# A graph layer on one core: another order for the first blocks, a block's list by one product, and pieces of blocks placed by running sums

## The chip, the cores and the metric

One core of a Trainium2 chip runs the whole program. The metric is the device time of one execution in microseconds (us); a run's profile gives the span of the profiled execution and what each engine did in it. The engines are TensorE (PE; its weight loads are PEld), VectorE (DVE), ScalarE (ACT), GpSimd (POOL) and SyncE (SP). SP, ACT and POOL also issue DMAs.

## What is computed

A layer of a graph network over 12,500 nodes with 64 features and 212,500 edges; `row` holds the edges' sources, `col` their destinations. The edge list is sorted by destination.

```python
h = relu(layernorm(x))
edge_in = concat([h[row], h[col], dist], axis=1)
e = silu(edge_in @ eW1 + eb1)
e = silu(e @ eW2 + eb2)
agg = segment_sum(e, row, num_segments=12500)
out = silu(concat([h, agg]) @ nW1 + nb1) @ nW2 + nb2
return x + out
```

## The kernel before

**Tables.** The first edge product is taken per node, not per edge: `ta` holds the source half of `h @ eW1` for every node, `tb` the destination half, both in DRAM, each number split in two parts that add up. A small table `tb0` holds the destination half for the first 2,048 nodes only, so that the first blocks need not wait for the whole of `tb`. This bulk work (load x, `norm`, `products`) is cut into small parts by generators; `feed` hands out one part at a time, between other work.

**Blocks.** The edges are taken in 208 blocks of 1,024; two blocks (a pair) share one window of 60 or so neighbouring destination nodes, which suffices since the list is sorted. `destinations()` makes each pair's list: `rowsD` holds every edge's destination relative to the window, `base_i` where the window begins. `sources()` splits the source of each edge into its bucket (one of 100) and its place in the bucket, turned so that edges lie on partitions. A block then goes through

- `load`: SP loads the pair's window rows from the table (`win`, L360), and the two edge-weight rows (`extra`, L335);
- `spread` (L344): TensorE copies the pair's list row to 64 partitions, twice, once for each half of the block (`bc`);
- `count`: VectorE finds each edge's rank within its bucket (`oh` L387, `each` L395, `terms` L412, `rank` L414, `to`) with two products on TensorE, and makes the one-hot `pick` (L376);
- `send`: TensorE gathers by a product (`qp`, L454), ScalarE copies it to `qs` (L466, L469; eight buffers), and POOL scatters 128 edges at a time to the bucket's next rows in DRAM (`q`, L476). That is 8 scatters a block, 1,661 in all.

`send_all` runs `send(s)` beside `count(s+1)` and `load(s+2)` and yields three times a block; each of these thirds is a *piece*.

**Steps.** The rows of `q` are filled in 14 levels (`LEVELS`). When all blocks that can reach a level are sent, its rows are read again, 25 batches a level, bucket by bucket: 450 steps of 512 edges. A step makes a one-hot of the places (`one` L605), turns it (`lr` L562), adds the source half and the gathered half (`pt` L576, L583), applies silu (L592), the second edge product (L622), silu (L626) and the sum by node (`seg` L636, `aggT` L647). With the last level the node part (`nodes`) follows for each batch and the rows of the output go out.

**Order.** TensorE, VectorE, ScalarE and SP run their instructions in the order in which the program writes them; each waits in that order. At the start an explicit list `order` interleaves the generators; then eight blocks run with four parts of `feed` to a piece, then the pieces that level 0 needs with three. In the main loop a list `turn` gives the order within a step; at four places of it (`None`, the *hooks*) pieces are placed. `marks` says how many pieces must stand before which hook, so that a level's rows are complete before its first batch is loaded, three blocks ahead; between two marks the pieces are spread evenly over the hooks.

**The bias tile.** `b2f` holds eb2 four times over on all partitions. It is loaded after the eighth block (L855), spread by a product with ones (L858) and copied back (L859).

Of the kernel before, what the change touches and what calls it, by code (L numbers as in the profile page):

```python
# [28 lines left out]
F32 = mybir.dt.float32  # L29
# [10 lines left out]
P = 128  # L40
L = 125
WL = 60
# [20 lines left out]
FILL0, FILL_EACH, FILL_LATE = 22, 2, 8  # L63
AFTER = mybir.DependencyInfo(mybir.DependencyClass.Sync, mybir.DependencyReason.DATA)
# [13 lines left out]
def tile_gnn(ctx: ExitStack, tc: tile.TileContext, x, src, dst, ew, eW1, eb1, eW2, eb2, nW1, nb1, nW2, nb2, out):  # L78
# [48 lines left out]
    NE, EARLY = 16, 30  # L127
# [9 lines left out]
    dstR = lp.tile([NP, PAIR], I32, name="dstR")  # L137
    f, sf, t = (lp.tile([NP, PAIR], F32, name=n) for n in ("f", "sf", "t"))
    fv = f.rearrange("p (g e) -> p g e", e=HALF)
    lo = lp.tile([NP, 4], F32, name="lo")  # L140
    ewR, ewH = (lp.tile([NP, PAIR], F32, name=n) for n in ("ewR", "ewH"))
    nc.vector.memset(srcR[96:NP, LAST:], N)
    nc.vector.memset(ewR[96:NP, LAST:], 0.0)
    ones = const.tile([1, P], F32, name="ones")
# [3 lines left out]
    nc.sync.dma_start(x0, x[: NE * P, :].rearrange("(p j) d -> p j d", j=NE))  # L148
# [5 lines left out]
    for to, v, queue in ((srcR, src, nc.sync), (ewR, ew, nc.scalar), (dstR, dst, nc.sync)):  # L154
        for p0, p1 in ((0, 96), (96, NP - 1)):
            queue.dma_start(to[p0:p1, :], vec(v, p0 * PAIR, p1 - p0, PAIR))
        queue.dma_start(to[NP - 1 : NP, :LAST], vec(v, (NP - 1) * PAIR, 1, LAST))
    last = bass.AP(tensor=dst.tensor, offset=dst.offset + E - FEW, ap=[[PAD, 1], [0, PAD // FEW], [1, FEW]])
    nc.scalar.dma_start(dstR[NP - 1 : NP, LAST:].rearrange("p (r e) -> p r e", e=FEW), last)
# [25 lines left out]
    nc.vector.scalar_tensor_tensor(same, plus, -float(HB), part, op0=OP.mult, op1=OP.add)  # L185
    nc.vector.tensor_scalar(plus, same, float(WL + 2), None, op0=OP.is_equal)
# [20 lines left out]
    rowsD = const.tile([NP, 2, 2, HALF], BF16, name="rowsD")  # L207

    tb0 = dram.tile([P * NE, 2 * H], F32, name="tb0")
    ta_buckets, tb_buckets = (t.rearrange("(l b) f -> l b f", b=NB) for t in (ta, tb))  # L210
# [21 lines left out]
    base_i = const.tile([1, NP], I32, name="base_i")  # L232
    NW = 3
    wins = [const.tile([P, 2, 2, 2, H], F32, name=f"win{i}") for i in range(NW)]
    for win in wins:
        nc.vector.memset(win, 0.0)
# [15 lines left out]

    def later_weights():

        nc.gpsimd.dma_start(w2, eW2)
# [48 lines left out]
    with ExitStack() as work:  # L304
# [23 lines left out]
        def load_rows(s):  # L328

            if s < nblocks:  # L330
                p, g = s // 2, s % 2
                if g == 0:
                    for a in range(2):
                        at = a * HB + WL
                        nc.sync.dma_start(extras[p % 2][at : at + 2], ews[:, p, :, a])  # L335

        def spread(s):

            if s < nblocks:
                p, g = s // 2, s % 2  # L340
                bc = mm.tile([P, HALF], F32, name="bc", tag="mm")
                for a in range(2):
                    of = identb[:NP, p : p + 1].to_broadcast([NP, HB])
                    nc.tensor.matmul(bc[a * HB : (a + 1) * HB], of, rowsD[:, a, g], start=True, stop=True)  # L344
# [344 lines left out]
        def first_rows(g):  # L689
# [6 lines left out]
            nc.sync.dma_start(  # L696
                tb0.rearrange("(p j) f -> p j f", j=NE)[:, g : g + G, :], got.rearrange("p g k h -> p g (k h)")
            )
# [43 lines left out]
        def destinations():  # L742

            lim = lp.tile([NP, 1], F32, name="lim")
            nc.vector.tensor_scalar(lim, part[:NP], EARLY / 2 - 0.5, float((NB - NE) * P), op0=OP.is_gt, op1=OP.mult)
            nc.vector.tensor_scalar(lim, lim, float(NE * P - SPAN), None, op0=OP.add)
            nc.scalar.copy(f, dstR)
            yield
            nc.vector.tensor_scalar(lo[:, 0:1], fv[:, 0, 0:1], lim, None, op0=OP.min)
            lot = mm.tile([1, NP], F32, name="lot", tag="mm")  # L750
            nc.tensor.transpose(lot, lo[:, 0:1], ident[:NP, :NP])
            for h in range(1, 4):
                nc.vector.tensor_scalar(lo[:, h : h + 1], lo[:, 0:1], float(h * STEP), None, op0=OP.add)
            yield
            nc.scalar.copy(base_i, lot)
            for g in range(2):
                nc.vector.tensor_tensor(
                    rowsD[:, :, g, :],
                    fv[:, 2 * g : 2 * g + 2, :],
                    lo[:, 2 * g : 2 * g + 2, None].to_broadcast([NP, 2, HALF]),  # L760
                    op=OP.subtract,
# [30 lines left out]
        def checks():  # L792

            ends = lp.tile([NP, 2, 4], F32, name="ends")
            for i, (op, sign, limit) in enumerate(((OP.max, 1.0, WL - 0.5), (OP.min, -1.0, 0.5))):
                nc.vector.tensor_reduce(ends[:, i, :], fv, AX.X, op)
                nc.vector.tensor_tensor(ends[:, i, :], ends[:, i, :], lo, op=OP.subtract)
                nc.vector.tensor_scalar(ends[:, i, :], ends[:, i, :], sign, limit, op0=OP.mult, op1=OP.is_gt)
                yield
            nc.vector.tensor_reduce(bad[:NP, 0:1], ends.rearrange("p i g -> p (i g)"), AX.X, OP.max)  # L800
# [17 lines left out]
        with listing:  # L818
            todo = groups()
            for _ in range(2):  # L820
                list(todo.pop(0))
            lists_, rows_, src0, src1, weights = destinations(), norm(x0, NE), sources(0), sources(1), edge_weights()
            made = [first_rows(g) for g in range(0, NE, G)]
            next(rows_)
# [233 lines left out]
```

## Time and profile before

| | |
|---|---|
| median of three runs | 2402.55 us (2399.72 to 2406.02) |
| the profiled execution | 2402.95 us |
| its span | 2401.2 us |
| mean granted clock of TensorE | 0.915 |
| first scatter begins | 43.5 us |
| last scatter begins | 2209.2 us |

A page of the profile lists the busy time of each engine, the span in 40 equal slices (busy tenths), the chain of waits that ended last, and groups of instructions as `line engine op out<-in`, with busy time, mean ns, and idle time ahead with what ended it (`<-`). A view of stretches gives busy time (and count) by engine, the granted clock, the DMA engines' busy share and GB/s. The timeline gives start, duration, engine and instruction.

### The profile page before, as it was taken

The numbers are of one execution on the slowest core, as the hardware profiler recorded it, in microseconds if no ns is written. First come the engines' busy times: TensorE is split into PE (matmuls) and PEld (weight loads), VectorE is DVE, ScalarE is ACT, GpSimd is POOL, SyncE is SP. The second block draws the span as 40 slices with busy tenths as digits, with TensorE's granted clock in tenths as the row PEclk, the third lists the DMA queues.
The fourth block names the chain that finished last, engine by engine and source line by source line (L and its number), as shares of the span: only waits on it lengthen the run. The fifth ranks groups of instructions, "written<-read, shape, count | busy, mean of one in ns | idle before, by whom it ended". The sixth has DMA issues, their size and how long they took to land.

```text
span 2401.2 us, 47870 instructions
## 1 busy us (share of the span) xinstructions
PE 2084.7 (87%) x17025; PEld 1909.0 (80%) x17025; DVE 1807.1 (75%) x2852; ACT 1316.8 (55%) x2861; POOL 1655.6 (69%) x1723
## 2 busy tenths in 40 slices
PE   3777887666688889988999999999999999999997
PEld 2555676655588788888888999998999999999885
DVE  7989977766678787776877667899988888875221
ACT  3333444333355566656666767666666666666543
POOL 5667777777777777777777766777777777776110
PEclk9555698877889999999999999999999999999999
DMA  5565877666677666777777777988888888888663
GB/s 161 210 235 212 274 227 236 209 209 220 210 250 253 209 225 221 225 236 255 258 259 247 264 251 254 294 262 255 269 269 275 266 267 279 263 270 269 207 187 92
DMA packets 238859, 572.33 MB, mean 238 GB/s; under 512 B 46346, under 2 KB 98534, under 8 KB 238097
## 3 DMA queue, kind: packets, MB, share of 16 engines
q1 hardware_dynamic: 154598, 390.24, 51.8%
q0 software_dynamic: 54080, 124.64, 14.2%
q10 hardware_dynamic: 29936, 54.31, 6.9%
q8 instruction: 138, 2.26, 0.4%
q14 instruction: 107, 0.88, 0.1%
HBM read 356.62 MB, written 212.35 MB: 237 GB/s over the span
## 4 chain that ended last, share of the span: by engine, by line
PE 43%; DMA 19%; POOL 10%; DVE 7%; issue 5%; ACT 4%; SPq 1%; ACTq 0%; POOLq 0%; DVEq 0%
DMA q<-qs,to 16%; PE seg L636 10%; POOL q L476 10%; PE p L622 10%; PE pt L583 9%; PE pt L576 5%; PE qp L454 4%; PE lr L562 3%; DMA out_dram<-os 2%; PE bc L344 1%; ACT qs L466 1%; DVE one L605 1%; SPq L124 1%; ACT e L592 1%; DVE rank L414 1%
## 5 line engine op out<-in xcount | busy, mean ns | idle before, releaser
L476 POOL DMA_INDIRECT q<-qs,to x1661 | 1615.7, 973 | 565.5 <-issue 398.4
L583 PE MATMUL pt<-oneT,a 125*128 125x128 f32 (+1 forms) x2800 | 433.9, 293 | 143.1 <-ACT oneT L567 142.1
L592 ACT ACTIVATE e<-pt 128x512 f32<-128x512 f32 x450 | 268.8, 597 | 477.4 <-PE pt L583 471.9
L622 PE MATMUL p<-w,e 128*128 128x128 f32 x3600 | 513.4, 287 | 0.0
L636 PE MATMUL seg<-one,e 128*128 128x125 f32 x3600 | 508.9, 285 | 0.2 <-DVE aggT L647 0.2
L583 PEld LDWEIGHTS pt<-oneT,a 125*128 125x128 f32 x2800 | 365.8, 198 | 159.5 <-ACT oneT L567 157.8
L622 PEld LDWEIGHTS p<-w,e 128*128 128x128 f32 x3600 | 457.6, 198 | 22.4 <-issue 22.4
L636 PEld LDWEIGHTS seg<-one,e 128*128 128x128 f32 x3600 | 445.3, 195 | 28.7 <-issue 27.3
L466 ACT COPY qs<-qp 128x512 f32<-128x512 f32 x418 | 244.5, 586 | 392.3 <-DMA q<-qs,to 276.1
L647 DVE TENSOR_TENSOR aggT<-aggT,seg 128x500 f32<-128x500 f32 x325 | 218.5, 672 | 210.1 <-PE seg L636 208.0
L454 PE MATMUL qp<-win,pick 128*128 128x256 f32 x1664 | 329.1, 325 | 28.3 <-DVE pick L376 10.8
L605 DVE TENSOR_TENSOR one<-misc,qt 128x500 f32<-128x500 f32 x450 | 302.7, 673 | 60.0 <-PE seg L636 33.1
L395 DVE TENSOR_REDUCE each<-oh 128x100 bf16<-128x800 bf16 x208 | 321.1, 1544 | 7.2
L454 PEld LDWEIGHTS qp<-win,pick 128*128 128x128 f32 x1664 | 254.1, 213 | 48.2 <-issue 15.1
L576 PE MATMUL pt<-ident,qt 128*128 128x128 f32 x1800 | 276.5, 277 | 8.3 <-ACT qs L466 7.9
L626 ACT ACTIVATE e<-p 128x512 f32<-128x512 f32 x450 | 268.7, 597 | 25.6 <-PE p L622 25.2
L567 ACT CAST oneT<-lr 125x512 fp32r<-125x512 f32 x450 | 264.7, 588 | 12.8 <-PE lr L562 12.4
L616 ACT COPY p<-b2f 128x512 f32<-128x512 f32 x450 | 267.2, 594 | 0.0
L576 PEld LDWEIGHTS pt<-ident,qt 128*128 128x128 f32 x1800 | 209.6, 143 | 23.7 <-issue 12.2
L414 DVE TENSOR_REDUCE rank<-terms 128x8 f32<-128x864 f32 x208 | 219.0, 1053 | 7.2
L376 DVE SCALAR_TENSOR_TENSOR pick<-bc,same,extra 128x512 fp32r<-128x512 f32 x208 | 154.6, 743 | 82.4 <-PE bc L344 54.3
L412 DVE TENSOR_TENSOR terms<-oh,misc 128x800 f32<-128x800 bf16 x208 | 203.6, 979 | 6.2 <-PE misc L400 5.9
(142 smaller groups left out, 1662.8 us busy)
## 6 DMA issues: line engine op xcount, KB each, us to landing
a<-ta SPq DMA_DIRECT2D x350, 512.0 KB
qt<-q SPq DMA_DIRECT2D x250, 288.0 KB
qt<-q SPq DMA_DIRECT2D x100, 576.0 KB
q<-zeros ACTq DMA_DIRECT2D x25, 1080.0 KB
q<-qs,to POOLq DMA_INDIRECT x1661
win<-tb SPq DMA_DIRECT2D x208, 120.0 KB
tb<-got SPq DMA_DIRECT2D x29, 512.0 KB
q<-zeros ACTq DMA_DIRECT2D x20, 720.0 KB
```

The source lines that it names most:

```text
L395: nc.vector.tensor_reduce(each, oh.rearrange("p t b -> p b t"), AX.X, OP.add)
L454: nc.tensor.matmul(qp[:, t % 2, :k], halves(pick[:, t * P : (t + 1) * P]), halves(win[:, :k, v]), start=v == 0, stop=v == 1,)
L466: nc.scalar.copy(qs[:, ts, :k, :H], qp[:, ts, :k, :])
L476: ins = nc.gpsimd.indirect_dma_start(out=q[:], out_offset=bass.IndirectOffsetOnAxis(ap=to[:k, j : j + 1], axis=0), in_=qs[:k, t % 2, a, :] ...
L576: nc.tensor.matmul(pt[:, t, :], qt[:, j, :H], ident, is_transpose=True, start=t == 0, stop=False, skip_group_check=True)
L583: nc.tensor.matmul(pt[:, cols, :], halves(a[:L, b, i * H : (i + 1) * H]), halves(oneT[:, cols, :]), start=False, stop=i == 1, skip_group_c ...
L592: nc.scalar.activation(e1, pt, AF.Silu)
L605: nc.vector.tensor_tensor(one.rearrange("p (b j) l -> p b j l", j=n), spots[:, None, None, :].to_broadcast(wide), loc[:, tiles[0][1] : til ...
L616: nc.scalar.copy(p2, b2f)
L622: nc.tensor.matmul(p2[:, t, :], e1[:, t, :], w2, start=False, stop=t == G - 1, skip_group_check=True)
L626: nc.scalar.activation(e2, p2, AF.Silu)
L636: nc.tensor.matmul(item[2][:, b, :], e2[:, t, :], one[:, t, :], start=j < G, stop=j >= G * (n - 1))
```

## The change

*The start.* The rows of the first four groups (512 nodes) go to a table of their own, `tb00`, which the first two pairs read; x is loaded in two parts to suit. The other three groups (`made[1:]`) become the first parts of `feed`, and the bulk's first loads of x follow the first window load. The edge-weight rows of block 0 are copied from `ewH` and `ewR` directly. `b2f` is loaded by POOL with the later weights and made before block 0's second product. `checks()` works in eight short reductions instead of two.

*The list.* The destinations lie as 128 partitions of two 512-edge halves, so that one product with a 128 x 128 selection `sel` (a copy on ScalarE, one for each pair) makes `bc`, in place of two products of 64 columns. Their load becomes eight DMAs of up to 32 partitions and two short ones, on SP, and four loads of single numbers (`firstR`) on ScalarE's queue.

*The placing.* Once `feed` is used up, pieces are no longer spread evenly. Two running sums stand for the time of TensorE (`now`) and of POOL (`sent`); a piece is placed at a hook while `sent - now` is under 30 us, and at the last hook ahead of a mark all that it asks for.

```diff
+PLAN_STEP, PLAN_PIECE, PLAN_SENT, PLAN_FETCH = {1: 3.4, 2: 2.95}, 0.55, 3.4, 8.0
+PLAN_AHEAD, PLAN_ROOM = 30.0, 36.0
...
         def spread(s):
...
-                for a in range(2):
-                    of = identb[:NP, p : p + 1].to_broadcast([NP, HB])
-                    nc.tensor.matmul(bc[a * HB : (a + 1) * HB], of, rowsD[:, a, g], start=True, stop=True)
+                nc.tensor.matmul(bc, sels[p % NW], rowsD[:, p // HB, g], start=True, stop=True)
...
         def load(s):
...
+                if s < 2 * FIRST_PAIRS:
+                    table, end = tb00, G * P
...
                 if g == 0:
+                    of = identb[:, p % HB :: HB][:, :, None].to_broadcast([P, 2, HB])
+                    nc.scalar.copy(sels[p % NW].rearrange("p (a m) -> p a m", a=2), of)
...
-            order = [rows_, weights, rows_, made[0], src0, made[0], src0, made[1], made[0], made[0], src0, made[1], lists_]
-            order += [made[2], made[1], made[1], src0, made[2], lists_, made[3], made[2], made[2], src0, made[3], lists_]
-            order += [made[3], made[3], src0, lists_, src1]
+            order = [rows_, rows_, made[0], src0, made[0], src0, weights, lists_, made[0], made[0], src0, src0, lists_]
+            order += [lists_, src0, src0]
             for part_ in order:
                 next(part_)
+            load(0)
+            load_rows(0)
+            for part_ in (count0, lists_, src1, count0):
+                next(part_)
...
-            feed = itertools.chain(itertools.islice(rest, 48), checks(), rest)
-            for _ in send_all(0, 2 * FIRST):
-                for _ in range(4):
+            feed = itertools.chain(turns(made[1:], 2), itertools.islice(rest, 40), checks(), rest)
+            for i, _ in enumerate(send_all(0, 2 * FIRST)):
+                for _ in range(2 if i < PIECES else 4):
                     next(feed, None)
...
+                    w, _, n, g = steps[min(max(k, 0), len(steps) - 1)]
+                    now = max(now, sent_by[opens[w]] + PLAN_FETCH) + PLAN_STEP[n] / hooks
...
-                        while done + 1 <= goal + 0.001:
-                            next(pieces, None)
-                            done += 1
+                    if ndp:
+                        goal = n1 if at + 1 == t1 else n0
+                    while done < total and (done + 1 <= goal + 0.001 or ndp and sent - now < PLAN_AHEAD):
+                        next(pieces, None)
+                        done += 1
+                        now = max(now + PLAN_PIECE, sent - PLAN_ROOM)
+                        sent = max(sent, now) + PLAN_SENT
+                        sent_by[done] = sent
```

More of the change, by code (lines that the diff above doesn't have):

```diff
@@ L143, in tile_gnn @@
     nc.vector.memset(ewR[96:NP, LAST:], 0.0)
+    nc.vector.memset(firstR, 0)
+    for a in range(2):
+        nc.vector.memset(dstR[a * HB + HB // 2 : (a + 1) * HB, NT - 1], (2 + a) * STEP)
     ones = const.tile([1, P], F32, name="ones")
@@ L153, in tile_gnn @@
     nc.scalar.dma_start(three[2:3, :], rows_of(eb1, 1))
[L154 removed]
+    for to, v, queue in ((srcR, src, nc.sync), (ewR, ew, nc.scalar)):
         for p0, p1 in ((0, 96), (96, NP - 1)):
@@ new lines, in destinations @@
+            lot = mm.tile([1, NT, P], F32, name="lot", tag="mm")
+            for T in range(NT):
+                nc.tensor.transpose(lot[:, T, :], base[:, T : T + 1], ident)
+            nc.vector.tensor_scalar(lo[:, :, 0], base, row[:, 1:2], None, op0=OP.add)
+            nc.vector.tensor_scalar(lo[:, :, 1], lo[:, :, 0], float(2 * STEP), None, op0=OP.add)
+            yield
+            nc.scalar.copy(base_i.rearrange("p (t r) -> p t r", r=HB), lot[:, :, :HB])
+            for T in range(NT):
+                if T:
+                    nc.scalar.copy(f[:, T], dstR[:, T])
@@ L851, in tile_gnn @@
         aggT = aggp.tile([P, NB, L], F32, name="aggT")
-        b2f = aggp.tile([P, G, H], F32, name="b2f")
-        eb2r = b2f[0:1, 0, :]
-        for t in range(G):
-            nc.sync.dma_start(b2f[0:1, t, :], rows_of(eb2, 1))
-        for _ in range(2):
-            p2 = p2p.tile([P, G, H], F32, name="p2")
-            nc.tensor.matmul(p2, ones, b2f[0:1], start=True, stop=True)
-            nc.scalar.copy(b2f, p2)
         ld2 = work.enter_context(tc.tile_pool(name="ld2", bufs=NQ))
@@ L884, in tile_gnn @@
             marks.append((hooks * (by - first), goal_of(w)))
+        opens = [PIECES * (end - 2 * FIRST) for _, end, _ in LEVELS]
+        now = PLAN_FETCH
+        sent_by = {n + 1: PLAN_SENT * (n + 1 - opens[0]) for n in range(done)}
+        sent = sent_by[done]
         at = 0
```

120 lines of the change are left out of this document (79 added, 41 removed).

## The prediction

> **What bounds the kernel now.** I read the page first: who is busiest, and where in the span.
>
> ```profile
> PE 2084.7 (87%) x17025; PEld 1909.0 (80%) x17025; DVE 1807.1 (75%) x2852; ACT 1316.8 (55%) x2861; POOL 1655.6 (69%) x1723
> ...
> POOL 5667777777777777777777766777777777776110
> ...
> L476 POOL DMA_INDIRECT q<-qs,to x1661 | 1615.7, 973 | 565.5 <-issue 398.4
> ```
>
> TensorE leads with 87%, but POOL's row is flat at 7 from the fourth slice to the thirty-sixth, apart from two 6s. A flat row at 0.76 of the time is a full engine when each instruction is followed by a fixed pause: one scatter takes 973 ns and 0.30 us of "issue" follow it, so the period is about 1.274 us. So the next view was the stretches, asked for line 476 alone, cut where the timeline shows POOL's gaps.
>
> ```profile
> 43.00:152.40 109.40, 64.90 (x64) 0.55 0.55 195
> 152.40:1417.00 1264.60, 962.70 (x991) 0.88 0.72 235
> 1417.00:1477.00 60.00, 32.32 (x34) 1.00 0.74 251
> 1477.00:2210.20 733.20, 555.81 (x573) 1.00 0.84 270
> 2210.20:2401.20 191.00, 0.00 (x0) 0.97 0.55 166
> ```
>
> (Columns: stretch, length, POOL busy and scatters, clock, DMA share, GB/s.) 991 scatters in 1264.6 us are 1.276 each, 573 in 733.2 are 1.280: POOL runs without a break there and sets the pace. In 43 to 152.4 there are 64 scatters, worth 81.6 us, so 27 us are lost; in 1417 to 1477 there are 34, worth 43.3, so 16.7 are lost. The span is thus 43.5 (the first scatter), 1661 periods, 27 + 17 of gaps, and a tail of 191 without scatters. Outside the gaps only an earlier start can shorten it.
>
> POOL's own rows in the timeline, with the wait that ended each gap:
>
> ```profile
> 43.52 1.90 POOL L476 DMA_INDIRECT q<-qs,to  x1 [14.59 <-ACT qs L469]
> ...
> 54.73 1.21 POOL L476 DMA_INDIRECT q<-qs,to  x1 [5.46 <-ACT qs L469]
> ...
> 113.57 0.97 POOL L476 DMA_INDIRECT q<-qs,to  x1 [6.36 <-ACT qs L469]
> ...
> 152.45 0.97 POOL L476 DMA_INDIRECT q<-qs,to  x1 [7.77 <-ACT qs L469]
> ...
> 1437.63 0.97 POOL L476 DMA_INDIRECT q<-qs,to  x1 [5.25 <-ACT qs L469]
> ...
> 2209.16 0.97 POOL L476 DMA_INDIRECT q<-qs,to  x1 [0.30 <-issue]
> ```
>
> In the first five ScalarE brought the block's rows late; the sixth is the last scatter. The rest of the argument asks why, at the start and at 1437.
>
> **The start: the way to the first scatter.** What ended last before 43.5:
>
> ```profile
> 4.52 9.04 SPq L156 DMA_DIRECT2D dstR<-in_dst_dram  x2
> ...
> 21.41 9.86 SPq L696 DMA_DIRECT2D tb<-got  x4
> ...
> 23.23 1.91 ACT L747 CAST f<-dstR 104x2048 f32<-104x2048 int32 x1
> ...
> 31.96 0.98 DVE L387 TENSOR_TENSOR oh<-misc,bkt 128x800 bf16<-128x800 f32 x1
> ...
> 36.95 0.17 DVE L416 TENSOR_SCALAR to<-rank 128x8 int32<-128x8 f32 x1
> ...
> 37.08 1.01 SPq L360 DMA_DIRECT2D win<-tb  x2
> ...
> 38.20 1.14 SPq L335 DMA_DIRECT2D extra<-ews  x4
> ...
> 40.42 0.75 DVE L376 SCALAR_TENSOR_TENSOR pick<-bc,same,extra 128x512 fp32r<-128x512 f32 x1 [3.30 <-DMA extra<-ews]
> ```
>
> SP writes four groups of table rows from 21.41 to 31.3, then the window load waits for all of them until 37.08, the list rows come behind it, and pick waits for those until 40.42. The first scatter is 3.1 us after pick's start. The change writes one group (tb00), so the window load follows the first write (21.4) and not the fourth; the rows 60 and 61 of block 0 come straight from ewH and ewR; three groups and the loads of x for the bulk work move behind it on SP. What is then late next is VectorE: destinations() needs dstR, then one pass for the rows, oh, each, the second rows pass, terms, rank, and pick. In the old kernel VectorE went from the start of oh (31.96) to the end of the ranks at 37.1, and f's cast stood on ScalarE at 23.23, behind copies for the bulk. In the new order half of f is cast at about that time, one rows pass follows, and oh can start some 6 us sooner, near 26; the 5.2 us from oh to the ranks and a second rows pass of 1.2 then end near 32.5. I put pick there and the first scatter at 36, 7.5 us earlier. Against it: 25 loads instead of 14 before the work, and ScalarE, in order, now issues five small ones (firstR, last) that wait for semaphores of earlier loads; behind them stand the square of the norm and all its copies. SP's dstR loads were held in the same way (9.04 us for two, at 4.52). If ScalarE is held to the end of that row, 13.6, the square comes 1 to 2 us late; I keep 0 to 4 as its range. So the first scatter comes between 33 and 41.
>
> **From the first scatter to block 8.** Two causes stand in the trace.
>
> ```profile
> 97.77 2.29 DVE L796 TENSOR_REDUCE ends<-f 104x4 f32<-104x2048 f32 x1
> ...
> 145.47 2.04 PE L858 MATMUL p<-b2f,ones 1*128 1x512 f32 x2 [4.83 <-DMA b2f<-in_L_gnn_eb_dram]
> ...
> 152.02 0.75 DVE L376 SCALAR_TENSOR_TENSOR pick<-bc,same,extra 128x512 fp32r<-128x512 f32 x1 [7.11 <-PE bc L344]
> ```
>
> The first is the bias tile: TensorE waits 4.83 us for it, ScalarE's copies follow, and everything in order behind stands; this is the 7.77 gap at 152.45. The change loads b2f early from POOL's queue and makes it while TensorE waits for pick anyway, so this gap goes; at worst its two products and copies, some 5 us, delay the first block by 2, which is in the range above.
>
> The second is VectorE. Its rows per block, then the bulk work's rows:
>
> ```profile
> L395 DVE TENSOR_REDUCE each<-oh 128x100 bf16<-128x800 bf16 x208 | 321.1, 1544 | 7.2
> ...
> L414 DVE TENSOR_REDUCE rank<-terms 128x8 f32<-128x864 f32 x208 | 219.0, 1053 | 7.2
> ...
> L387 DVE TENSOR_TENSOR oh<-misc,bkt 128x800 bf16<-128x800 f32 (+1 forms) x209 | 203.9, 976 | 2.4 <-ACT bkt L781 2.4
> ...
> L412 DVE TENSOR_TENSOR terms<-oh,misc 128x800 f32<-128x800 bf16 x208 | 203.6, 979 | 6.2 <-PE misc L400 5.9
> ...
> L376 DVE SCALAR_TENSOR_TENSOR pick<-bc,same,extra 128x512 fp32r<-128x512 f32 x208 | 154.6, 743 | 82.4 <-PE bc L344 54.3
> ...
> L227 DVE TENSOR_TENSOR rows_a<-ab,rows_a 128x256 f32<-128x256 f32 x50 | 18.8, 417 | 1.3 <-ACT rows_a L224 0.7 <-issue 0.5
> ...
> L666 DVE TENSOR_TENSOR cen<-xs,mean 128x768 f32<-128x768 f32 (+1 forms) x9 | 8.1, 899 | 0.3
> ```
>
> The five passes are 5.3 us; with the three small ones a block costs about 6. A norm has four passes like L666 and small ones, about 4.2; a subtraction 0.42. In the order of the built programs, between pick of block 0 and pick of block 8, the old kernel has 40 subtractions and 5 norms, the new one 34 and 4; both have the checks (4.6 plus small ones, say 5.4) and the second half of sources (about 6 with its wait). So old: 8 x 6 + 16.8 + 21 + 5.4 + 6 = 97 us, from 41.2 to 138; new: 48 + 14.3 + 17 + 5.4 + 6 = 91, from 33.3 to 124. VectorE, not POOL (8 x 10.2 = 82), paces these blocks in both. The old kernel's block 8 could have scattered at about 141 and did at 152.45 after the bias stall and ScalarE's waits for norms (its copies stand in order behind a norm's square: 113.57). The new one: 124 + 3, plus some 3 for such waits, is 130. Bounds: 122 (no such waits, first scatter at 33) and 142 (all of them, first scatter at 41). **Block 8 comes 22 us earlier, 10 to 30.**
>
> The checks are split into eight short passes over two blocks, the same total. Of the steps moved later, the products end at block 22 instead of 20 in the built order; the tables are needed at block 30, so nothing waits.
>
> **The steps and the gap at 1437.** From the order of the built programs I counted half blocks (copies to qs) placed by the start of each level's steps. The old kernel spreads them evenly between two marks: 26 within the 50 steps of level 5, 47 in levels 6 and 7. The new one puts 35 within level 5 and 40 after; from level 8 on both are alike. In levels 0 to 4 it places at the plan's pace and the rest in one run before the mark (8, 32, 13, 10 and 10 halves); POOL is full there in both, so this moves nothing. Who was full at 1437?
>
> ```profile
> 1417.00:1477.00 60.00, 58.79 (x541) 57.03 (x538) 42.98 (x67) 41.95 (x87) 32.32 (x34) 1.00 0.74 251
> 1477.00:2210.20 733.20, 717.74 (x6493) 685.94 (x6492) 625.50 (x966) 464.09 (x999) 555.81 (x573) 1.00 0.84 270
> ...
> 1896.39 0.23 PE lr L562 x4
> ...
> 1900.26 0.34 PE bc L344 x2
> ```
>
> TensorE was (58.79 of 60): it did steps while POOL starved, and had 15.5 us to spare in the 733 us behind. Moving four blocks forward fills POOL's 16.7 us, but then TensorE must do the rest with almost no idle time: 1.2 + 15.5 spare, plus what the one list product saves. That product streams 512 columns once, as the four lr products do in 0.23 us, in place of 0.34: 0.1 a block, 9 us over the last 87 blocks. So between 0 and 16.7 come back; I take 12, near the upper end, because levels 8 to 11 already ran with POOL full beside the same mix. sel's copy on ScalarE (104 of 128x128, each under the 0.60 that 128x512 takes below) finds 36% of ScalarE free there: nothing.
>
> **The tail.** After the last scatter the first e of the last level comes 17 us later, one step behind the one before:
>
> ```profile
> 2222.60 0.60 ACT L592 ACTIVATE e<-pt 128x512 f32<-128x512 f32 x1 [1.32 <-PE pt L583]
> ...
> 2226.01 0.60 ACT L592 ACTIVATE e<-pt 128x512 f32<-128x512 f32 x1 [1.33 <-PE pt L583]
> ```
>
> A step is 3.4 us here, as the plan has it. No line of the tail changes; 191 stays.
>
> **Sum.** The profiled execution took 2402.95 us (span 2401.2), 0.4 above the median of the three runs. 2402.95 - 22 - 12 = 2369; POOL's sum says the same: block 8 at 130, 1597 scatters x 1.277 = 2039, tail 191, 1.75 around the span, and 4 to 5 of what stays of the gap make 2366. I say **2368**.
>
> **Rivals.**
> - TensorE becomes the bound from level 5 on: the 16.7 us of POOL are filled, but come back as TensorE's lag, and the last level starts late. For it: 97.9% busy already. Only the start counts: 2381. Chance 0.17.
> - The start doesn't come: the longer chain of loads holds ScalarE, VectorE's norms (two stand together before pick of block 3) hold its copies, and block 8 comes at 145 or later. Against: the bias stall is gone in any case. 2403 - 7 - 10 = 2386. Chance 0.12.
> - Slower. The plan's clock runs faster than the real engines: from level 5 on there is no run before a mark that makes up for it, so each step that takes longer than its 3.4 or 2.95 (plus pieces) takes that time from POOL. There are 225 such steps; from 0.15 us each the gain is gone, with 0.25 it is 2368 + 56 = 2424. Against: the even spread stood at the same density in levels 8 to 11 and lost nothing. Chance 0.06.
> - The runs of pieces leave TensorE cold.
>
> ```profile
> 256.00:274.00 18.00, 12.65 (x56) 9.47 (x56) 17.62 (x25) 7.69 (x17) 13.57 (x14) 0.52 0.78 264
> 274.00:294.00 20.00, 17.33 (x154) 16.15 (x154) 19.59 (x31) 11.23 (x26) 15.27 (x16) 1.00 0.92 298
> ```
>
> With blocks alone the granted clock was 0.52, and 4 us after the first step it was 1.00. Five levels begin so; a half-speed start of 4 us loses 2 us of TensorE, 10 in all, if POOL's queue (three blocks ahead at a mark, about 30 us, less 17 until the first e) didn't cover it: 2378. Chance 0.05. The Trainium skill, "TensorE: Matmul & The Clock Gate", section Part 1, says that an idle window of about 3.4 us halves the clock and a busy one restores it; by that rule the five would be an estimated 8.5 us. The trace agrees with it.
>
> **How the numbers follow.** The forecast has 0.6. Its own bounds are 22 (10 to 30) and 12 (0 to 16.7): 2356 to 2393 at the ends together. The range of 2352 to 2390 holds it, and the second, third and fifth case; what is left out is the slower case and the ends. A measurement of this kernel can tell 0.3%, 7 us: slower has the third rival's 0.06; 0.04 of the two rivals above it goes to the same, for a start and a level 5 that fail together; 0.90 is left for faster.
>
> **What would show it.** First scatter near 36, the 65th near 130, and no wait of TensorE for b2f's load. POOL at 48 scatters in every 60 us from 180 to 2150, 1417 to 1477 included; if that stretch is full but a later one falls under 47, the first rival holds. The time from the last scatter to the end stays 191; if it grows, TensorE had a backlog. Wrong altogether if POOL has new gaps behind the starts of levels 1 to 5.

## The result, and the profile after

| | before | after |
|---|---|---|
| median of four runs, us | 2403.45 (2399.72 to 2406.02) | 2367.89 (2365.88 to 2368.72) |
| span of the profiled execution | 2401.2 | 2365.5 |
| mean granted clock of TensorE | 0.915 | 0.892 |
| first scatter | 43.5 | 42.2 |
| 65th scatter (block 8) | 152.5 | 136.3 |
| 968th scatter (last of the first 121 blocks, end of level 5's rows; "block 121" below) | 1305.4 | 1289.4 |
| last scatter | 2209.2 | 2173.3 |
| from there to the end | 192.0 | 192.2 |

The ratio is 0.9854, 95% interval [0.9839, 0.9868]: 36 us less. The forecast was 2368.0, and the sum behind it was 22 us from the start and 12 from the middle. The rows say 16 and 20. That the total fits to 0.2 us is luck: the two errors cancel, so most of what follows is about them.

The page of after, in the three lines that answer to those of before:

```profile
PE 2028.7 (86%) x16818; PEld 1902.7 (80%) x16818; DVE 1814.7 (77%) x2865; ACT 1333.0 (56%) x2966; POOL 1655.9 (70%) x1724
...
POOL 5777777777777777777777777777777777776110
...
L515 POOL DMA_INDIRECT q<-qs,to x1661 | 1616.1, 973 | 526.5 <-issue 396.9
```

POOL's row is now flat from the second slice on, the two 6s are gone, and the scatter still takes 973 ns. So POOL sets the pace as before, with fewer holes. The stretches of line 515 alone (length, POOL busy and scatters, clock, DMA share, GB/s):

```profile
42.00:124.00 82.00, 57.10 (x56) 0.69 0.53 188
124.00:1390.00 1266.00, 962.04 (x990) 0.82 0.72 240
1390.00:1450.00 60.00, 45.60 (x47) 1.00 0.86 280
1450.00:2174.40 724.40, 551.37 (x568) 1.00 0.84 272
```

56 scatters in the first 82 us are worth 71.3 at 1.274, so 11 us are lost there; before, 27 were lost up to block 8. The third stretch covers the place where before had 34 scatters in 60 us: it holds 47. The last one has 568 in 724.4, 1.275 each; before it was 1.280.

The same execution with all engines (PE, PEld, DVE, ACT, POOL busy and counts, then clock, DMA share, GB/s):

```profile
1289.40:1411.00 121.60, 118.59 (x1083) 116.03 (x1083) 99.01 (x151) 87.23 (x188) 92.61 (x96) 1.00 0.83 280
1411.00:1477.00 66.00, 64.62 (x594) 63.20 (x593) 54.10 (x85) 48.06 (x104) 50.14 (x53) 1.00 0.83 265
1477.00:2174.40 697.40, 680.62 (x6248) 668.01 (x6247) 589.86 (x911) 453.56 (x992) 530.84 (x547) 1.00 0.84 273
2174.40:2365.50 191.10, 170.54 (x1363) 149.14 (x1361) 47.25 (x87) 84.77 (x169) 18.19 (x25) 0.97 0.55 167
```

TensorE is busy for 863.8 of the 885 us up to the last scatter, 97.6%, yet the tail has not grown: TensorE keeps up.

Why the first scatter came at 42.2 and not at 36 stands in the timeline of after:

```profile
6.87 9.13 ACTq L176 DMA_DIRECT2D firstR<-in_dst_dram  x4
...
13.86 1.23 DVE L705 TENSOR_TENSOR cen<-x,mean 128x1024 f32<-128x1024 f32 x1
...
16.77 1.06 ACT L706 ACTIVATE x<-cen 128x1024 f32<-128x1024 f32 x1 [11.94 <-DMA firstR<-in_dst_dram]
...
25.90 1.05 ACT L795 CAST f<-dstR 128x1024 f32<-128x1024 int32 x1
26.09 4.53 POOL L837 TENSOR_TENSOR ewR<-ewR,ewH 104x2048 f32<-104x2048 f32 x1 [3.59 <-ACT ewH L836]
...
26.98 4.72 DVE L810 TENSOR_TENSOR rowsD<-f,lo 128x1024 bf16<-128x1024 f32 x1 [1.18 <-ACT f L795]
...
31.62 0.98 DVE L426 TENSOR_TENSOR oh<-misc,bkt 128x800 bf16<-128x800 f32 x1
...
31.80 3.06 SPq L368 DMA_DIRECT2D extra<-ewR  x2
...
34.04 1.21 DVE L810 TENSOR_TENSOR rowsD<-f,lo 128x1024 bf16<-128x1024 f32 x1
...
37.10 2.07 PE L896 MATMUL p<-b2f,ones 1*128 1x512 f32 x2 [0.68 <-ACT b2f L897]
...
37.74 0.17 DVE L455 TENSOR_SCALAR to<-rank 128x8 int32<-128x8 f32 x1
...
39.06 0.75 DVE L415 SCALAR_TENSOR_TENSOR pick<-bc,same,extra 128x512 fp32r<-128x512 f32 x1 [1.16 <-DMA extra<-ewR]
...
42.16 1.91 POOL L515 DMA_INDIRECT q<-qs,to  x1 [10.50 <-ACT qs L508]
```

ScalarE's issues of the small loads took 9.13 us, and the square of its first norm came at 16.77, 1.7 us after its input `cen` was ready (15.09). The cast of half of `f` came at 25.90. The pass that makes `rowsD` took 4.72 us where the same pass took 1.21 at 34.04; the long one lies beside POOL's subtraction of the edge weights, and ends 1.1 us after it (31.70 and 30.62), as if it had run only then. VectorE was done with the ranks at 37.91, and `pick` waited another 1.16 for the list row that the subtraction makes. The last hold is the list row; the largest is the pass.

### The profile page after: what moved, and what is told of

Same layout as the page of the kernel before. It is cut to its first block, busy times and chain, and to the rows that moved or that the text cites. A ratio compares the mean times of both kernels' runs of the same rounds, so it can differ in the third digit from the quotient of the medians.

```text
span 2365.5 us, 47589 instructions
## 1 busy us (share of the span) xinstructions
PE 2028.7 (86%) x16818; PEld 1902.7 (80%) x16818; DVE 1814.7 (77%) x2865; ACT 1333.0 (56%) x2966; POOL 1655.9 (70%) x1724
## 4 chain that ended last, share of the span: by engine, by line
PE 58%; DMA 12%; DVE 11%; POOL 6%; issue 4%; ACT 2%; SPq 2%; POOLq 0%; DVEq 0%; ACTq 0%
PE seg L675 15%; PE p L661 14%; PE pt L622 10%; DMA q<-qs,to 8%; PE pt L615 6%; POOL q L515 6%; PE qp L493 6%; PE lr L601 4%; DMA out_dram<-os 3%; DVE each L434 1%; DVE oh L426 1%; PE bc L379 1%; DVE rank L453 1%; DVE terms L451 1%; DVE pick L415 1%
## 5 line engine op out<-in xcount | busy, mean ns | idle before, releaser
L675 PE MATMUL seg<-one,e 128*128 128x125 f32 x3600 | 502.3, 283 | 2.0 <-DVE aggT L686 1.7
L661 PE MATMUL p<-w,e 128*128 128x128 f32 x3600 | 498.6, 282 | 0.0
L661 PEld LDWEIGHTS p<-w,e 128*128 128x128 f32 x3600 | 449.9, 195 | 9.9 <-issue 9.2
L622 PE MATMUL pt<-oneT,a 125*128 125x128 f32 (+1 forms) x2800 | 423.0, 289 | 14.4 <-DMA a<-ta 8.5
L493 PEld LDWEIGHTS qp<-win,pick 128*128 128x128 f32 x1664 | 268.5, 224 | 202.6 <-ACT qs L505 121.6
L493 PE MATMUL qp<-win,pick 128*128 128x256 f32 x1664 | 347.7, 340 | 93.5 <-ACT qs L505 60.6
L622 PEld LDWEIGHTS pt<-oneT,a 125*128 125x128 f32 x2800 | 356.8, 194 | 18.3 <-issue 9.7
L615 PEld LDWEIGHTS pt<-ident,qt 128*128 128x128 f32 x1800 | 215.3, 144 | 19.7 <-ACT qs L505 11.0
L426 DVE TENSOR_TENSOR oh<-misc,bkt 128x800 bf16<-128x800 f32 (+1 forms) x209 | 203.8, 975 | 2.4 <-ACT bkt L831 2.4
```

The costliest lines, as they stand in the source:

```text
L493: nc.tensor.matmul(qp[:, t % 2, :k], halves(pick[:, t * P : (t + 1) * P]), halves(win[:, :k, v]), start=v == 0, stop=v == 1,)
L615: nc.tensor.matmul(pt[:, t, :], qt[:, j, :H], ident, is_transpose=True, start=t == 0, stop=False, skip_group_check=True)
L622: nc.tensor.matmul(pt[:, cols, :], halves(a[:L, b, i * H : (i + 1) * H]), halves(oneT[:, cols, :]), start=False, stop=i == 1, skip_group_c ...
L661: nc.tensor.matmul(p2[:, t, :], e1[:, t, :], w2, start=False, stop=t == G - 1, skip_group_check=True)
L675: nc.tensor.matmul(item[2][:, b, :], e2[:, t, :], one[:, t, :], start=j < G, stop=j >= G * (n - 1))
```

## The experiments

The first four kernels and the kernel before beside them ran on a chip on which the kernel before took 39% longer (3341.13 us), so their ratios don't compare with the later ones. The first three were therefore run again on a second chip, where the kernel before took 2400.39 us; experiment 8 stands against this number too, and 9 to 12 against 2404.07, on a third chip.

**1. Even spread.** Start and list product of after, the old spreading of pieces:

```diff
-                    if ndp:
-                        goal = n1 if at + 1 == t1 else n0
-                    while done < total and (done + 1 <= goal + 0.001 or ndp and sent - now < PLAN_AHEAD):
+                    while done < total and done + 1 <= goal + 0.001:
```

> The changed kernel, but pieces spread evenly between marks as before; the new start and the one list product stay. Theory (the scatters set the pace, the two halves of the gain add up): the gap of POOL in level 5 comes back, 16 to 20 us, so 2384 to 2388, with some 34 scatters instead of 47 in 60 us near 1400 to 1460, and the start as in the changed kernel. Rival (the late gain is TensorE's, from the shorter list product, not from the placing): under 5 us are lost, 2368 to 2373.

3326.77 us, ratio 0.9955 [0.9931, 0.9979].

**2. Two products for the list.** The expectation speaks of the even spread beside the two products; the kernel that ran is after with two products and keeps the new placing.

```diff
-                nc.tensor.matmul(bc, sels[p % NW], rowsD[:, p // HB, g], start=True, stop=True)
+                for a in range(2):
+                    half = slice(a * HB, (a + 1) * HB)
+                    nc.tensor.matmul(bc[half], sels[p % NW][:, half], rowsD[:, p // HB, g], start=True, stop=True)
```

> The changed kernel with the even spread (as the run before this one), and the list again by two products of 64 columns, from the same selection. Theory: POOL sets the pace and TensorE has some 20 us of idle time from level 5 on, so 0.1 us a block costs nothing: within 3 us of the run with the even spread, 2384 to 2390. Rival (TensorE is the bound there): 9 us or more on top, 2394 and up.

3512.93 us, 1.0507 [1.0470, 1.0545].

**3. Placing only.** The kernel before with the new placing, the old start and the two products:

```diff
+PLAN_STEP, PLAN_PIECE, PLAN_SENT, PLAN_FETCH = {1: 3.4, 2: 2.95}, 0.55, 3.4, 8.0
+PLAN_AHEAD, PLAN_ROOM = 30.0, 36.0
...
+                    if ndp:
+                        goal = n1 if at + 1 == t1 else n0
+                    while done < total and (done + 1 <= goal + 0.001 or ndp and sent - now < PLAN_AHEAD):
```

> The kernel before with the new placing alone; old start, two products. Theory: the gap in level 5 is filled, 16 to 20 us, so 2383 to 2387, and the start is the old one (first scatter 43.5, the 65th at 152). Rival (TensorE needs the shorter product to keep up): 8 us or less are won, 2395 and up.

3527.50 us, 1.0548 [1.0506, 1.0589].

**4. The bias tile late.** After, with `b2f` loaded and made behind the eighth block, as before:

```diff
-        nc.gpsimd.dma_start(b2f[0:1], bass.AP(tensor=eb2.tensor, offset=eb2.offset, ap=[[0, 1], [0, G], [1, H]]))
...
+        for t in range(G):
+            nc.sync.dma_start(b2f[0:1, t, :], rows_of(eb2, 1))
```

> The changed kernel, but the bias tile is loaded and spread after the eighth block, as before. Theory: the stall of 7.5 us in POOL returns before block 8 or 9, and the first scatter comes some 2 us sooner since the two products leave the stretch ahead of it; 2373 to 2376. Rival (VectorE paces the first blocks anyway, so the stall only takes the place of its lag): within 2 us of 2368.

3506.72 us, 1.0500 [1.0463, 1.0538]. What it was to price, some microseconds at block 8, drowns in the 5% that each of experiments 2 to 4 shows, and it was not run again; experiment 12 prices its two products alone. The three that have the new placing are 5% slower than the kernel before there; the one without it is not. The waits of POOL (what for, us in all, times, longest), first of the even spread, then of the placing alone:

```profile
POOL q L515 <- ACT qs L508: 996.1, 192, 12.3
```

```profile
POOL q L478 <- ACT qs L471: 1204.3, 193, 17.0
```

On that chip POOL stands waiting for rows in both, 200 us more with the placing. The chain of waits of the second kernel, a piece of it (start, length, what):

```profile
2015.03 0.14 ACT qs L471
2015.17 5.72 another core or an unknown queue
2020.91 0.60 ACT e L594
```

After a copy stand 5.72 us that the profile can't put down to any engine; such pieces are 31% of the chain from 2000 to 2030 us. The even spread has them as well, 17% of its whole chain. So the engines there don't run at the plan's figures, and it may be that what orders the pieces by those figures loses where an even spread doesn't. That this is the cause of the 5% is argued from the waits, not shown; why that chip was slower stays open.

**5 to 7. The edits of experiments 1 to 3 on the second chip.** First the even spread, as in experiment 1:

> The changed kernel with the pieces spread evenly between marks as before; new start and one list product stay. Theory (the scatters set the pace and the parts of the gain add up): the gap of POOL in level 5 returns, 16 to 20 us, so 2384 to 2388, and the last scatter comes as much later. Rival (the late gain is TensorE's, from the shorter list product): 2368 to 2373.

2380.52 us, 0.9915 [0.9898, 0.9931]. The waits of POOL's gap of before are back, in its timeline:

```profile
1419.36 0.97 POOL L515 DMA_INDIRECT q<-qs,to  x1 [5.04 <-ACT qs L508]
...
1433.71 0.97 POOL L515 DMA_INDIRECT q<-qs,to  x1 [3.94 <-ACT qs L508]
...
1446.82 0.97 POOL L515 DMA_INDIRECT q<-qs,to  x1 [3.19 <-ACT qs L508]
```

Its last scatter is 898.8 us behind block 121's, against 883.9 in after and 903.8 in before. So the placing is worth 15 us there, and the one product without it 5. By the medians, each against the kernel before beside it, the placing is worth 15.7, a little under the 16 to 20 expected; the rival, 2368 to 2373, is out.

The placing alone, as in experiment 3:

> The kernel before with the new placing alone. Theory: 16 to 20 us are won, 2383 to 2387, with the old start (65th scatter at 152) and a full POOL from 1290 on. Rival (TensorE needs the shorter product to keep up): 8 us or less are won, 2395 and up.

2393.71 us, 0.9976 [0.9966, 0.9985]: 6.7 us won, so the theory's 16 to 20 fail and the rival's "8 us or less" holds. The list in two products, as in experiment 2, so with the new start and placing:

> The changed kernel, but the list of a block again by two products of 64 columns from the same selection; the new placing stays. Theory (POOL sets the pace, TensorE has some 20 us idle in the 885 us from the end of block 121 to the last scatter): 0 to 4 us slower, 2368 to 2372. Rival (TensorE is the bound from there on): 0.1 us for each of 87 blocks and their step's restart on top, 9 us or more, 2377 and up.

2378.23 us, 0.9904 [0.9888, 0.9921]: 10 us above after, and 13 when each stands against its own kernel before, so here too the rival holds and not the theory. The late stretches of the placing alone, up to the last scatter and behind it, and below them those of the two products:

```profile
1306.60:2191.90 885.30, 871.53 (x7883) 835.56 (x7881) 740.23 (x1137) 574.63 (x1226) 673.79 (x694) 1.00 0.82 270
2191.90:2393.60 201.70, 183.10 (x1488) 162.34 (x1486) 52.21 (x95) 92.92 (x185) 19.10 (x26) 0.97 0.56 174
```

```profile
1291.30:2176.40 885.10, 870.88 (x7866) 834.83 (x7865) 739.18 (x1137) 581.31 (x1265) 673.63 (x694) 1.00 0.82 270
2176.40:2379.20 202.80, 184.27 (x1503) 163.92 (x1502) 52.84 (x97) 93.92 (x186) 19.15 (x26) 0.97 0.56 175
```

In both, POOL gets its 694 scatters out in 885 us, as in after: the placing fills POOL's gap by itself. But the tail is 202 and 203 us where after has 192, and the kernels with one product 188 to 193 (experiment 11 apart): TensorE, with two products a block, is some 10 us behind when POOL is done. This is the first rival of the prediction, made to happen: the gap is filled and comes back as TensorE's lag. From the four kernels, each against the kernel before that ran beside it: placing alone 6.7 us, start and product 19.9, start and placing 22.2, all three 35.6. With the start worth 16 (the rows of the result's table), the product alone is worth 4, the placing alone 7, and the two together 20. Neither wins much without the other.

**8. The start: the loads and the pass.** After, with `firstR` and the last short load issued from POOL's queue, and `rowsD` made from one tile and a column:

```diff
-            nc.scalar.dma_start(firstR[a * HB : a * HB + n, T : T + 1], shown(T * HB, n, 0, [[1, 1]]))
+            nc.gpsimd.dma_start(firstR[a * HB : a * HB + n, T : T + 1], shown(T * HB, n, 0, [[1, 1]]))
...
-                nc.vector.tensor_tensor(
-                    rowsD[:, T], f[:, T], lo[:, T, :, None].to_broadcast([P, 2, HALF]), op=OP.subtract
-                )
+                for g in range(2):
+                    nc.vector.tensor_scalar(rowsD[:, T, g], f[:, T, g], lo[:, T, g : g + 1], None, op0=OP.subtract)
```

> The changed kernel with two stalls of its start taken away: the five small loads of destinations go out on POOL's queue, so ScalarE no longer waits behind them, and rowsD is made by passes with one operand from memory and a number for each partition, in place of a pass over two tiles. Theory: the pass of 4.72 us waited for POOL's subtraction that ran beside it and needed a path that POOL held; with one operand it takes under 1 us for each half, the norm's square starts at 15 and not 16.8, and the first scatter comes 3 us or more sooner, unless the list rows of block 0, which also wait for POOL's subtraction, come last then: first scatter 37 to 40, and 2363 to 2367 in all. Rival (the pass was slow for another reason, such as its own shape): rowsD still ends at 31 or later, first scatter at 41 to 42.

2349.79 us, 0.9786 [0.9769, 0.9802], which is 15 us better than after, when each stands against its own kernel before. It is not by the start, and neither theory nor rival had it: the first scatter comes at 41.7, the 65th at 135.2. In its timeline the two passes still take 4.36 us beside POOL's subtraction and 0.87 later:

```profile
25.30 4.52 POOL L836 TENSOR_TENSOR ewR<-ewR,ewH 104x2048 f32<-104x2048 f32 x1 [0.79 <-ACT ewH L835]
...
26.20 4.36 DVE L811 TENSOR_SCALAR rowsD<-f,lo 128x512 bf16<-128x512 f32 x2 [1.19 <-ACT f L795]
...
32.89 0.87 DVE L811 TENSOR_SCALAR rowsD<-f,lo 128x512 bf16<-128x512 f32 x2
...
38.58 0.75 DVE L415 SCALAR_TENSOR_TENSOR pick<-bc,same,extra 128x512 fp32r<-128x512 f32 x1 [2.17 <-DMA extra<-ewR]
```

`pick` still waits for the list row. The gain is in the group of the scatters:

```profile
L515 POOL DMA_INDIRECT q<-qs,to x1661 | 1598.3, 962 | 529.3 <-issue 401.0 <-DMA q<-qs,to 38.5 <-ACT qs L508 22.0
```

962 ns each where after has 973: 11 ns by 1661 are 18 us, and the two spans differ by 17.1.

**9 and 10. Each half of experiment 8 alone.** The loads on POOL's queue:

> The changed kernel with one edit of the fourth experiment alone: the five small loads of the start (four of firstR, one into dstR) are issued from POOL's queue instead of ScalarE's; the pass that makes rowsD is the changed kernel's. Open is why the kernel with both edits ran 16 us faster although its first scatter came only 0.5 us sooner: its scatters took 962 ns each instead of 973. Theory A: the loads are the cause (they change what stands ahead of the scatters on POOL's queue of transfers): here scatters of 962 ns, a period of 1.262 to 1.264 us, 2350 us. Theory B: the one-operand pass is the cause: here 973 ns, a period of 1.274 and 2365 to 2368 us. In both the first scatter stays between 41.5 and 42.5.

2352.15 us, 0.9782 [0.9766, 0.9798]. The passes of one tile and a column:

> The changed kernel with the other edit of the fourth experiment alone: rowsD is made by two passes of 128x512 with one tile and a column of factors instead of one pass of 128x1024 with two tiles; the loads stay on ScalarE's queue. By theory A (the loads shorten the scatter) 973 ns and 2365 to 2368 us; by theory B 962 ns and 2350 us. If both this and the kernel with the loads alone show 962 ns, any change of the program ahead of the scatters does it; if neither does, it is the two together, and its cause stays open.

2369.20 us, 0.9857 [0.9841, 0.9874]. The scatters of the first, then of the second:

```profile
L515 POOL DMA_INDIRECT q<-qs,to x1661 | 1603.5, 965 | 527.2 <-issue 400.3 <-DMA q<-qs,to 37.8 <-ACT qs L508 21.7
```

```profile
L515 POOL DMA_INDIRECT q<-qs,to x1661 | 1615.5, 973 | 526.5 <-issue 398.3 <-DMA q<-qs,to 35.6 <-ACT qs L508 22.0
```

The loads carry it and the pass does nothing: theory A, as far as these two go. The profiled execution of the second took 2360.89 us, 8 under the median of its four, so its row may not stand for the other three.

**11. The plan's clock fast.** The slower rival, made to happen:

```diff
-PLAN_STEP, PLAN_PIECE, PLAN_SENT, PLAN_FETCH = {1: 3.4, 2: 2.95}, 0.55, 3.4, 8.0
+PLAN_STEP, PLAN_PIECE, PLAN_SENT, PLAN_FETCH = {1: 2.7, 2: 2.35}, 0.55, 3.4, 8.0
```

> The changed kernel with the plan's cost of a step lowered from 3.4 and 2.95 us to 2.7 and 2.35 us, so that the plan's clock runs fast by 0.6 to 0.7 us a step: the slower rival of the prediction made on purpose. The placed pieces then lie later among the steps: by the end of level 6 the order is 8 half blocks of scatters behind the changed kernel's, after level 7 it is 11 behind, and each level ends in a run of pieces. A half block is 5.1 us of POOL, and the plan keeps some 30 us ahead. If POOL's supply is what the placing buys, POOL idles 10 to 30 us between 1300 and 1700, the last scatter comes as much later, and the time is 2375 to 2400. If the plan's figures hardly matter, as the rival with TensorE as the bound would have it, the time stays at 2366 to 2370.

2451.63 us, 1.0195 [1.0178, 1.0212]: 2% slower than the kernel before, with start and product of after in place. Stretches up to the last scatter and behind it, and some of POOL's rows in the timeline:

```profile
1306.90:2251.10 944.20, 883.96 (x7785) 863.12 (x7784) 739.88 (x1136) 581.84 (x1266) 674.02 (x694) 0.94 0.77 253
2251.10:2453.80 202.70, 183.78 (x1494) 163.08 (x1492) 52.71 (x96) 93.54 (x186) 19.16 (x26) 0.97 0.56 174
```

```profile
1549.06 0.97 POOL L515 DMA_INDIRECT q<-qs,to  x1 [2.66 <-ACT qs L508]
...
1563.15 0.97 POOL L515 DMA_INDIRECT q<-qs,to  x1 [4.19 <-ACT qs L508]
```

POOL's waits for ScalarE's rows from 1280 us on (us in all, times, longest):

```profile
POOL q L515 <- ACT qs L508: 64.0, 38, 4.2
```

The same 694 scatters take 944 us instead of 884: POOL waits for the rows 38 times in 87 blocks, up to 4.2 us. TensorE has idle time too (60 of 944 us), its granted clock falls to 0.94, and 10 us of lag stand behind the last scatter. I read this as the run of pieces at each mark coming too late for POOL and delaying the steps behind it; the rows show the waits, not this order. My expectation had 10 to 30 us; POOL's starving was right and the size too small, since I let the 30 us that the plan keeps ahead pay once for the whole, and set nothing down for the levels before 5 (17.5 us by block 121) and the tail.

**12. The three holds of the start.** Experiment 8 with the subtraction on VectorE, block 0's list rows ahead of its window, and the bias products behind the first eight blocks:

```diff
-            nc.gpsimd.tensor_tensor(ewR, ewR, ewH, op=OP.subtract)
+            yield
+            nc.vector.tensor_tensor(ewR, ewR, ewH, op=OP.subtract)
...
+            load_rows(0)
             load(0)
-            load_rows(0)
...
-            for _ in range(2):
-                p2 = p2p.tile([P, G, H], F32, name="p2")
...
                 for _ in range(2 if i < PIECES else 4):
                     next(feed, None)
+            for _ in range(2):
+                p2 = p2p.tile([P, G, H], F32, name="p2")
```

> The fourth experiment's kernel with three more edits at the start: the difference of the edge weights is taken on VectorE instead of POOL, after the table's first rows; block 0's list rows are issued ahead of its window; and the two products that spread the bias are made behind the first eight blocks. In the changed kernel and in the fourth experiment the first scatter waited for the list row that comes from that difference (product of the list at 39.06 and 38.58), with rowsD's pass stretched to 4.4 to 4.7 us while POOL made the difference, and with the bias products in TensorE's queue up to 38.0. Theory: these three are what kept the first scatter at 42 and not 36: rowsD's passes take 0.9 us, the list product comes at 34 to 36 and the first scatter at 36.5 to 38.5, with the time 3 to 5 us under the fourth experiment's: about 2345. Rival: the window's rows or ScalarE's other work hold the first scatter instead (first scatter 40 to 42, time as in the fourth experiment).

2367.53 us, 0.9846 [0.9830, 0.9863]. Its timeline:

```profile
25.28 2.29 DVE L837 TENSOR_TENSOR ewR<-ewR,ewH 104x2048 f32<-104x2048 f32 x1 [0.97 <-ACT ewH L835]
...
28.22 0.88 DVE L811 TENSOR_SCALAR rowsD<-f,lo 128x512 bf16<-128x512 f32 x2
...
35.23 0.75 DVE L415 SCALAR_TENSOR_TENSOR pick<-bc,same,extra 128x512 fp32r<-128x512 f32 x1
...
38.33 1.91 POOL L515 DMA_INDIRECT q<-qs,to  x1 [9.90 <-ACT qs L508]
...
132.59 2.07 PE L906 MATMUL p<-b2f,ones 1*128 1x512 f32 x2 [0.68 <-ACT b2f L907]
...
136.31 0.75 DVE L415 SCALAR_TENSOR_TENSOR pick<-bc,same,extra 128x512 fp32r<-128x512 f32 x1 [3.71 <-PE bc L379]
...
136.86 0.97 POOL L515 DMA_INDIRECT q<-qs,to  x1 [4.99 <-ACT qs L508]
```

The theory of the start holds: with the three holds gone the passes take 0.88, `pick` waits for no list row, and the first scatter comes at 38.3, inside the 36.5 to 38.5 expected. The time does not: about 2345 was expected. The start buys nothing at block 8 (136.9), since the bias products now stand in TensorE's queue there, and POOL waits 4.99 us for them; that was the third edit's price, which I had not set down. Which of the three edits moved the first scatter was not separated. And the short scatter of experiments 8 to 10 is gone: 974 ns again, with the loads still on POOL's queue. So theory A, the loads as such, falls with this run: they are not enough.

## Why the prediction was right, and where it was not

**The limit: right.** POOL's period of 1.274 us with no break sets the pace after as before. 56 + 990 + 47 + 568 scatters fill their stretches but for 11 us at the start and 5 in the long one. My sign of a full POOL, 48 scatters in every 60 us, was set too high: 60 us hold 47.1 periods, and 1390 to 1450 has its 47. Behind 201 us no scatter of after starts more than 1.6 us after the one ahead of it, so there are no new gaps.

**The first scatter: wrong by 6.** I put 36 (33 to 41); it came at 42.2, outside. The profiled executions of experiments 5 and 11, with the same start, have 40.6 and 41.0, just inside. So one execution differs from the next by 1.5 us, and none comes near 36.

The step that failed is "oh can start some 6 us sooner, near 26": it started at 31.62. I took the cast of `f` over from the old kernel, "at about" 23.23, and it came at 25.90; and I priced a pass of `rowsD` at the 1.2 us that it takes alone, where the first took 4.72 beside POOL's subtraction. From there the forecast was right, 6.3 us from `oh` to the end of the ranks for 6.4. Behind them the list row, which I had copied "straight" without asking when POOL's 4.5 us subtraction is done, held `pick` for another 1.16. So the 6.6 us by which `pick` came late (39.06 for 32.5) are some 2 of the cast, 3.5 of the pass and 1.2 of the list row.

ScalarE held by its small loads was in the text, with 0 to 4 us, and was not what counted. The square did come 4.4 later (16.77 against 12.39), but `cen` was ready 2.7 later, so 1.7 are the loads'. With the loads moved, in experiments 8 and 9, the first scatter came at 41.7 and 41.9, inside the 40.6 to 42.2 of the unmoved ones. Experiment 12 took the subtraction from beside the pass and the wait from `pick`, and got 38.3.

The Trainium skill, "GPSIMD Engine Reference", section 1 (Specifications), says that GpSimd shares SBUF interfaces with VectorE, with contention for VectorE instructions of two SBUF inputs or in a mode that uses two ports; the trace of after agrees (4.72 against 1.21 us). Changing the pass to one tile and a column did not help in experiment 8 (4.36 against 0.87), so what the operands contribute was not shown here, nor in which mode that pass ran.

**From the first scatter to block 8: right.** 94 us in the sum (36 to 130), 94.1 in the trace (42.2 to 136.3). From `pick` of block 0 to `pick` of block 8 the sum had 91 and the trace has 90.5. That VectorE alone paces these blocks is not shown: it is busy for 80.2 of the 90.5 us. The bias stall is gone: POOL's four long pauses in this part are 2 to 3 us each, the last at 126, and TensorE waits for no load of the bias tile.

**The gap at 1437: right in kind, too small.** I said 12, with 16.7 as the upper end; block 121 to the last scatter went from 903.8 to 883.9, 19.9. The step that failed is the bound, which counted only the gap. POOL did not run "without a break" behind it: three more pauses, at 1478, 1560 and 1571, cost 3 us. That is what the 1.280 for each of the 573 scatters in 733.2 us holds; at 1.274 they are 730.0, and these 3.2 us were there to win as well. Of TensorE's budget, 1.2 + 15.5 of spare time and 9 from the product, the 9 are borne out: without the product 10.6 us of lag stand in the tail (202.8 against 192.2). The spare time is not: TensorE was to be left with almost none, but it has 21.2 us idle in the 885 of after, and 17.2 in the 903.8 of before. Its busy time there fell by 22.8 us (886.6 to 863.8), more than the product's 9; what the rest is stays open.

**The tail: right**, 192.2 for 191 to 192. In the profiled executions of experiments 5, 8, 9, 10 and 12, all with one product, it is 187.7 to 192.7.

**The rivals.** TensorE as the bound came true only where the product was left out: 2378.2, for 2381 worked out. "The start doesn't come" did not; 16 of 22 us came. The slower case is real but not at these figures: with the plan's step 0.6 to 0.7 us short it costs 84 us against after, and none at 3.4 and 2.95. Its price in the prediction, each step's shortfall charged to POOL, would make 50 x 0.6 + 175 x 0.7 = 152 us from level 5 on; 60 were measured there before the last scatter and 10 behind it; that the runs at the marks give the rest back is a guess. TensorE did get colder ahead of level 5, 0.82 in 124 to 1390 us, where before it had 0.88 in 152 to 1417; POOL lost nothing by it (from block 8 to block 121 it took 1153.1 us, and 1152.9 before), so the cover of 30 us in the last rival held.

## What to carry to other kernels

A filled gap is won only if the next engine has the time: ask for the spare time of the runner-up in the same stretch, and look for it in the tail, where its lag comes out. Two edits may each be worth little and together much; undo them one at a time before judging either. And a first result's time is that of its latest input: write down when each input is made, the short copies as well, and on which engine its maker stands beside what.

## What the runs showed of the hardware

A scatter's duration goes with the program and not with the place in it. Its mean in the one profiled execution of each kernel is 973 ns in before, after and experiment 10, 974 to 975 in experiments 5 to 7, 11 and 12, 971 to 974 on the slow chip, and 962 and 965 in experiments 8 and 9. The median is the same in the first and the second half of a run (969 ns in after, 958 in experiment 8). Since POOL is the limit, 11 ns are 18 us, more than the placing is worth. The two short ones have the five small loads on POOL's queue; so has experiment 12, with one POOL instruction fewer ahead of the scatters, and there it is 974. What sets it stays open. The 2 ns between 973 and 975 are 3 us, so small differences between kernels here can come from it alone. The kernels of experiments 8 and 9 are faster than after, at 2.1% and 2.2% under the kernel before, by an effect that I can use but not explain.
